# Loading one weight as mirrored 32x32 squares and turning it on VectorE, in a float32 two-layer sequence kernel

## The chip, the cores and the metric

The kernel runs on one core of one Trainium2 chip. Its time is the device time of one execution in microseconds; before the change it is the median of three executions, 1170.36 us. The engines are TensorE (PE, matrix products; PEld is its loading of the stationary operand), VectorE (DVE), ScalarE (ACT), GpSimd (POOL) and SyncE (SP, which here only issues transfers). Sixteen DMA engines move data between the chip's large memory and the on-chip memory of 128 partitions. SP, ACT and POOL each have a queue of transfers on these same sixteen engines.

## The reference

There are 4 sequences x of 512 tokens and 512 features, all in float32. The first layer, with V = 512 and HID = 2048:

```
q, k, v  = x @ Wq, x @ Wk, x @ Wv
attn     = softmax(q @ k.T * V**-0.5)
attn_out = (attn @ v) @ Wp + bp
cms      = gelu(attn_out @ cW1 + cb1) @ cW2 + cb2 + one_hot(code)
modifier = gelu([attn_out, cms] @ mW1 + mb1) @ mW2 + mb2
y        = clip(x + cms + modifier, 0, 1)
```

The second layer picks one of three small adapters for each sequence (`stream` is the index of the adapter):

```
h   = gelu(y @ W_down[stream] + b_down[stream]) @ W_up[stream] + b_up[stream]
out = layernorm(y + h) * ln_w[stream] + ln_b[stream]
```

## The kernel before

**Products by seven.** Every large product is cut into 2x2 blocks and computed with seven block products instead of eight (Winograd's form of Strassen's scheme). That needs four sums of the left operand's blocks (s1 to s4, made by `weight_sums`, L196) and four of the right operand's (t1 to t4). The wide products of the later layers use the scheme twice, one inside the other; their weights' sums (c1, c2, m1, m2) are made by GpSimd early in the kernel, in units, stored in the large memory and loaded again when their product comes. The generator `expansion` (L420) holds these units in order; `steps(expanding, n)` (L473) lets it issue the next n pieces.

**Attention.** The sequences are taken in two pairs. Wq and Wk are folded once into one matrix, Wq Wk^T, and Wv and Wp into another, Wv Wp (`folded`, L744). For each pair the code in L912 to L984 makes, in this order, u = x times the first matrix (`pair_product`, L933, both sequences at once), for the first pair the fold of Wv and Wp, two softmaxes (L773), two products that mix the rows of x by the attention (L970), and the product with the second matrix (L982). The results `attn` go to the large memory and come back as the right operand of c1, after which c2, m1, m2 and the adapters follow for each pair.

**The fold of Wv and Wp** needs Wv transposed, in `wv_t`, which is the tile mod[0], and four sums of its blocks, which take the place of the raw Wv in slot[2]. The raw Wv and Wp are loaded at the start by SP's queue, behind Wq and the first two x (L149 to L151). `then[7]` (L932) hangs the transposes of Wv into u's product, behind its block product p = 7: sixteen 128x128 transposes on TensorE into four banks of its accumulator memory (`transposed`, tile tr_ps, L489), each bank copied to wv_t by ScalarE and used by VectorE for the sums (`left_from_psum`, L720).

**u's product** takes the block products p in the order 1, 2, 5, 6, 7, 4, 3 for two row blocks r (`seven`, L591). After p = 6 and p = 7 VectorE adds kept results to the accumulators (L547): p = 4 goes into the accumulator of p = 7 and so cannot start on a row before VectorE's sum of p = 7 for that row has read it. The right operands of p = 5 and 6 lie in mod[0], those of p = 7 and 4 in mod[1].

**GpSimd's early work,** in its own order: the left sums of the first x (L923), the loads of the first half of cW1 (L234, four transfers) and of x 2 and 3 (L142), the first c1 unit, the right sums of Wp for the fold (L931, operations on L741), the rest of that unit, small constants (L524), the second c1 unit with the loads of cW2, and then the first c2 unit. The left sums of the second x stand in the program behind the first softmax (L951), since their place, wslot[0], holds a softmax operand until then; a scheduler, which orders each engine's instructions by estimated times, mixed them with the c2 unit. `tc.keep_in_program_order` pins an instruction against that scheduler; it is used for some groups of sums.

**Adapters.** `load_adapter` (L1486) fetches, by indirect transfers on GpSimd's queue, four pieces of W_down, two of b_down (bd), four of b_up (bu), two of W_up, and ln_w and ln_b for one sequence. It is called twice near the end of each pair. The bd and bu pieces have small tiles of their own, so nothing but their indices holds them back, and the scheduler put the first ones at 63 us and 22 more at 340 to 377 us. During c1 of the second pair GpSimd also makes sums of c1's right operands (L1079 and L1087 to L1090); in its queue they stand behind the first pair's adapter loads.

Of the kernel before, what the change touches and what calls it, by code (L numbers as in the profile page):

```python
# [1 line left out]

# [16 lines left out]
def kernel(  # L19
# [125 lines left out]
    def rows_of(t):  # L145
        return t.rearrange("p (c n) -> p c n", c=4)

    x_places = (big[0], big[1], rows_of(slot[6]), rows_of(slot[7]))
    x_rows = [load_x(b, nc.sync, x_places[b]) for b in range(2)]  # L149
    wv = weight((nc.sync, nc.sync), Wv, slot[2])  # L150
    wp = weight((nc.sync, nc.sync), Wp, slot[3])  # L151


    bias_src = (bp, cb1, cb2, mb1, mb2)
    counts = [v.shape[0] // P for v in bias_src]
# [37 lines left out]
        nc.tensor.matmul(idle_ps[:, :P], lhsT=zeros, rhs=zeros, start=True, stop=True)  # L193


    def weight_sums(a11, a12, a21, a22, s1, s2, s3, s4, eng=None):  # L196
        eng = eng or nc.gpsimd
        eng.tensor_tensor(s1, a21, a22, ALU.add)
        eng.tensor_tensor(s2, s1, a11, ALU.subtract)
        eng.tensor_tensor(s3, a11, a21, ALU.subtract)  # L200
        eng.tensor_tensor(s4, a12, s2, ALU.subtract)  # L201

    def token_sums(b11, b12, b21, b22, t1, t2, t3, t4, eng=None, pinned=False):
        eng = eng or nc.vector
# [144 lines left out]
    def expand(unit, raw, pairs, last, then):  # L349


        src, is_first, dst, u = unit
        raw = [t.rearrange("p (c n) -> p c n", c=4) for t in raw]
        a11, a12, a21, a22 = (
            raw[0][:, :, :256], raw[1][:, :, :256], raw[0][:, :, 256:], raw[1][:, :, 256:]
        )
        one, two, three = pairs
        s1, s2, s3 = (block(t[:, :1024]) for t in pairs)

        def tt(out_, a, b, op):  # L360
            nc.gpsimd.tensor_tensor(out_, a, b, op)

        def keep(p, t):
            nc.gpsimd.dma_start(out=dst[p, u], in_=t)

        tt(s1, a21, a22, ALU.add)
        tt(s2, s1, a11, ALU.subtract)
        tt(s3, a11, a21, ALU.subtract)

        def plain(*blocks):  # L370
            for p, a, t in blocks:
                inner_sums(a, t[:, 1024:])
                keep(p, t[:, 1024:])
                yield

        def fourth(s4, t):
            inner_sums(s4, t[:, 1024:])
            nc.gpsimd.dma_start(out=block(dst[3, u][:, :1024]), in_=s4)
            nc.gpsimd.dma_start(out=dst[3, u][:, 1024:], in_=t[:, 1024:])
            yield  # L380

        def full(*sums):
            for p, t in sums:
                inner_sums(block(t[:, :1024]), t[:, 1024:])
                keep(p, t)
                yield

        if last is not None:  # L390
            yield from plain((2, a12, one), (1, a11, three), (4, a22, two))
            tt(block(last), a12, s2, ALU.subtract)
            then()
            yield from full((5, one), (7, three), (6, two))
            yield from fourth(block(last), one)
        else:
            yield from plain((2, a12, one))
            tt(a12, a12, s2, ALU.subtract)
            yield from fourth(a12, three)
            yield from plain((1, a11, two), (4, a22, one))  # L400
            then()
            yield from full((5, one), (7, three), (6, two))
# [40 lines left out]
    def inner_weights(src, is_first, store, p, u):  # L443
# [26 lines left out]
            5: s[:, 0], 6: s[:, 1], 7: s[:, 2], 3: s[:, 3],  # L470
        }

    def steps(gen, n):  # L473
        for _ in range(n):
            next(gen, None)

    expanding = expansion()

# [186 lines left out]
        s1, s2, s3, s4 = (s[:, k] for k in range(4))  # L665
        return {1: a11, 2: a12, 3: s4, 4: a22, 5: s1, 6: s2, 7: s3}

    def left_sums(t, s):
        weight_sums(*halves(t), *(s[:, k] for k in range(4)))

    def right_operand(t, s):

# [43 lines left out]

    def sums_in(t):
        return t.rearrange("p (k c n) -> p k c n", k=4, c=2)

    def left_from_psum(t, s):  # L720

        s1, s2, s3, s4 = (s[:, k] for k in range(4))

        def finish(d, ps):
            nc.scalar.copy(t[:, d, :], ps)
            c = d % 2
            if d < 2:
                minus(s3[:, c], ps[:, :256], t[:, c, 256:])
            else:
                minus(s2[:, c], ps[:, 256:], s3[:, c])  # L730
                add(s1[:, c], ps[:, 256:], t[:, c, 256:])
                minus(s4[:, c], ps[:, :256], s2[:, c])

        return finish

    def right_sums(t, w):

# [174 lines left out]
    for pair in range(B // 2):  # L912
        s0, s1 = 2 * pair, 2 * pair + 1
        xT, t_x = places(pair)
        t_x = [sums_in(flat(t)) for t in t_x]
        u = big[4 - 2 * pair : 6 - 2 * pair]
        attn = big[6:8]
        s_u = [sums_in(wslot[k]) for k in range(2)]
        s_x = [sums_in(wslot[k]) for k in (2, 0)]
        t_p = t_x  # L920
        then = {}
        wv_t = mod[0]
        left_sums(x_rows[s0], s_x[0])  # L923
        if pair:
            s_x[1] = sums_in(flat(attn[1]))
            left_sums(x_rows[s1], s_x[1])
        if pair == 0:

            steps(expanding, 2)
            s_v = sums_in(slot[2])  # L930
            rhs_wp = right_sums(wp, w_vp)  # L931
            then[7] = [lambda: transposed(chunks(wv), wv_t, left_from_psum(wv_t, s_v))]  # L932
        pair_product(lhs_qk, begun, u, beside=beside_u(s_u, u), then=then)  # L933
        if pair == 0:

            lhs_vp = folded(
                left_operand(wv_t, s_v), rhs_wp, w_vp, s_v, order=(1, 5, 6, 2, 7, 3, 4)
            )
        steps(expanding, 6 if pair else 4)
        pT, mix = u, xT  # L940

        def turn(k):
            transposed(lambda t: mod[k][:, t, :], pT[k], right_from_psum(pT[k], t_p[k]))

        for k in range(2):
            softmax(
                k, left_operand(u[k], s_u[k]), right_operand(xT[k], t_x[k]),
                {7: [lambda: turn(0)]} if k else None,
            )
            if k == 0 and pair == 0:  # L950
                left_sums(x_rows[s1], s_x[1])  # L951
        for k in range(2):
            if k == 0:
                def keep(half, tokens, ps):
                    nc.scalar.copy(
                        mix[0][:, 2 * half : 2 * half + 2, 256 * tokens : 256 * tokens + 256], ps
                    )
            else:
                operands, take = second_operand(*mix, mod)
                held = []  # L960

                def keep(half, tokens, ps):

                    if (half, tokens) == (1, 1):
                        held.append(ps)
                        return
                    take(half, (slice(0, 2), slice(256 * tokens, 256 * tokens + 256)), ps)
                    if (half, tokens) == (0, 1):
                        take(1, (slice(0, 2), slice(256, 512)), held[0])

            small_product(
                left_operand(x_rows[s0 + k], s_x[k]), right_operand(pT[k], t_p[k]), keep,
                {7: [lambda: turn(1)]} if k == 0 else None,
                nc.scalar.copy if k else nc.vector.tensor_copy,
            )
            steps(expanding, 6)
        then = {}
        if pair == 0:
            begun = {}
            then = {6: [lambda: first_operand(1)()], 4: [lambda: begun.update(both_operands(1))]}  # L980

        pair_product(lhs_vp, operands, attn, bp_c, then=then, at=pT[0] if pair else None)  # L982
        for k in range(2):
            nc.scalar.dma_start(out=attn_kept[s0 + k], in_=attn[k])  # L984
# [489 lines left out]
    bd_rows = b_down.rearrange("e (k o) -> (e k) o", o=1)  # L1474

    def gathered(dst, rows, idx):
        nc.gpsimd.indirect_dma_start(
            out=dst,
            out_offset=None,
            in_=rows,  # L1480
            in_offset=bass.IndirectOffsetOnAxis(ap=idx, axis=0),
        )
# [3 lines left out]
    def load_adapter(b, w, aff):  # L1486
        wd = w[:, : NV * BN].rearrange("p (c n) -> p c n", c=NV)
        wu = w[:, NV * BN : NV * BN + NB * V].rearrange("p (c n) -> p c n", c=NB)
        aff = aff[:, : 2 * V].rearrange("p (k n) -> p k n", k=2)
        bd = small.tile([P, NB], F32, name="bd")  # L1490
        bu = small.tile([P, NV], F32, name="bu")
        for c in range(NV):
            gathered(wd[:, c, :], wd_rows, idx_d[:, b, c : c + 1])
        for c in range(NB):
            gathered(bd[:, c : c + 1], bd_rows, idx_u[:, b, c : c + 1])
        for c in range(NV):
            gathered(bu[:, c : c + 1], bu_rows, idx_d[:, b, c : c + 1])
        for c in range(NB):
            gathered(wu[:, c, :], wu_rows, idx_u[:, b, c : c + 1])
        for i, rows in enumerate((ln_w, ln_b)):  # L1500
            gathered(aff[:, i, :], rows, idx_e[:, b : b + 1])
        return wd, wu, bd, bu, aff

    def with_bias(y, bu, y1):
# [297 lines left out]
```

## Time and profile before

| | |
|---|---|
| Three timed runs | 1168.99, 1170.36, 1171.34 us |
| Median | 1170.36 us |
| Profiled execution, its own time | 1169.93 us |
| Its span in the profile | 1168.2 us |
| TensorE busy, matrix products | 1158.7 us (99%) |
| VectorE busy | 893.8 us (77%) |
| ScalarE busy | 293.2 us (25%) |
| GpSimd busy | 588.6 us (50%) |
| Transposes of Wv on TensorE (tr_ps, 16) | 42.9 to 48.8 us of the span |
| Left sums of the second x on GpSimd | 95.9 to 111.8 us |
| Bias gathers on GpSimd, longest run | 339.7 to 377 us |

The profile follows one execution. Times are microseconds from the start of its span. A group or a row names the line of the kernel, the engine, the operation and its tiles (out<-in); "idle before" is how long the engine had stood still and what ended that. The chain of waits is followed back from the last instruction: at each step to what released it, or to the instruction before it on its engine. A matrix product of float32 with 256 columns appears as two records.

### The profile page before, as it was taken

How to read it: one execution, taken by the hardware profiler on the slowest of the kernel's cores; microseconds unless marked ns; L12 is line 12 of the kernel's file. 1: busy time of each engine (PE TensorE's matmuls, PEld its weight loads, DVE VectorE, ACT ScalarE, POOL GpSimd, SP SyncE). 2: the span in 40 equal slices, each digit the busy share in tenths (PEclk: the TensorE clock that was granted, in tenths of full speed). 3: DMA queues.
4: the chain of work that ended last, by engine and by line, in shares of the span. 5: the costliest groups of instructions: out<-in, count | busy, mean ns of one | idle time of the engine just before them, and what ended most of it. 6: DMA issues, size and time to landing. Idle time of an engine off the chain costs nothing.

```text
span 1168.2 us, 13723 instructions
## 1 busy us (share of the span) xinstructions
PE 1158.7 (99%) x4989; PEld 927.4 (79%) x4989; DVE 893.8 (77%) x1215; ACT 293.2 (25%) x535; POOL 588.6 (50%) x652
## 2 busy tenths in 40 slices
PE   9999999999999999999999999999999999999997
PEld 8588558657468888888888887778888888888875
DVE  5755655587699967899699956689994588689956
ACT  4244315236520000012310027271000003220014
POOL 4989999988897058982200636972000001242101
PEclk9999999999999999999999999999999999999999
DMA  9742784897766588896847662135745454594701
GB/s 336 268 139 100 297 323 176 307 382 253 300 240 245 185 282 313 322 328 263 258 157 279 191 215 90 64 143 179 299 132 188 168 216 180 176 307 165 246 6 73
DMA packets 81283, 256.80 MB, mean 220 GB/s; under 512 B 7956, under 2 KB 38976, under 8 KB 65984
## 3 DMA queue, kind: packets, MB, share of 16 engines
q1 hardware_dynamic: 56864, 152.98, 36.4%
q0 software_dynamic: 21968, 93.37, 22.7%
q10 hardware_dynamic: 2384, 9.57, 2.1%
q8 instruction: 40, 0.66, 0.2%
q14 instruction: 27, 0.22, 0.1%
HBM read 186.69 MB, written 66.06 MB: 216 GB/s over the span
## 4 chain that ended last, share of the span: by engine, by line
PE 94%; DVE 2%; POOL 1%; DMA 1%; issue 1%; DVEq 0%
PE i L1406 29%; PE i L1306 26%; PE sum L1148 9%; PE sum L703 9%; PE sum L637 8%; PE c L1238 6%; PE down_ps L1512 2%; PE up_ps L1531 2%; PE tr_ps L489 1%; DMA wslot<-in_L_cond_mW 1%; PE up_ps L1526 1%; DVE slot L206 1%; DVE hidden L547 1%; PE tr_ps L868 0%; PE idle_ps L193 0%
## 5 line engine op out<-in xcount | busy, mean ns | idle before, releaser
L1306 PE MATMUL i<-slot,wslot 128*128 128x256 f32 x1184 | 261.4, 379 | 1.3 <-DVE part L1010 1.2
L1306 PEld LDWEIGHTS i<-slot,wslot 128*128 128x128 f32 x1184 | 224.7, 190 | 32.8 <-issue 1.8
L1406 PE MATMUL i<-slot,wslot 128*128 128x256 f32 x896 | 202.5, 379 | 0.0
L1406 PEld LDWEIGHTS i<-slot,wslot 128*128 128x128 f32 x896 | 170.2, 190 | 23.1
L1017 ACT COPY first<-i 128x256 f32<-128x256 f32 (+1 forms) x56 | 26.7, 477 | 516.0 <-PE i L1406 255.6
L1406 PE MATMUL i<-hidden,wslot 128*128 128x256 f32 x576 | 132.2, 379 | 0.0
L1406 PEld LDWEIGHTS i<-hidden,wslot 128*128 128x128 f32 x576 | 109.4, 190 | 15.7 <-issue 1.0
L1010 DVE TENSOR_TENSOR part<-i,part 128x512 f32<-128x512 f32 (+1 forms) x156 | 90.5, 591 | 37.7 <-PE i L1306 25.4
L1039 ACT ACTIVATE hidden<-hidden,bias 128x512 f32<-128x512 f32 x128 | 83.9, 716 | 81.3 <-DVE hidden L547 71.3
L1688 POOL DMA_DIRECT2D slot<-xT_kept x4 | 2.7, 683 | 152.9 <-PE i L1306 152.9
L1148 PE MATMUL sum<-mod,wslot 128*128 128x256 f32 x288 | 66.7, 379 | 0.2 <-DVE sum L547 0.2
L206 DVE TENSOR_TENSOR slot<-hidden 128x1024 f32<-128x1024 f32 x46 | 61.3, 1332 | 0.0
L1148 PEld LDWEIGHTS sum<-mod,wslot 128*128 128x128 f32 x288 | 54.6, 190 | 7.9 <-DVE sum L547 0.6
L1691 POOL TENSOR_TENSOR cms<-cms,slot 128x512 f32<-128x512 f32 x16 | 24.4, 1548 | 71.3 <-PE i L1306 41.1
L1010 DVE TENSOR_TENSOR part<-i,first 128x512 f32<-128x512 f32 (+1 forms) x62 | 36.3, 589 | 29.0 <-PE i L1306 17.7
L547 DVE TENSOR_TENSOR sum<-sum,wslot 128x512 f32<-128x512 f32 x48 | 33.3, 696 | 31.5 <-PE sum L703 19.6
L206 DVE TENSOR_TENSOR slot<-hidden,slot 128x1024 f32<-128x1024 f32 x46 | 56.8, 1234 | 0.3
L1238 PE MATMUL c<-slot,wslot 128*128 128x512 f32 x128 | 55.3, 592 | 0.0
L547 DVE TENSOR_TENSOR hidden<-part,hidden 128x2048 f32<-128x2048 f32 x20 | 54.6, 2732 | 0.5
L703 PE MATMUL sum<-hidden,wslot 128*128 128x256 f32 x232 | 53.4, 380 | 0.6 <-POOL wslot L201 0.6
L703 PEld LDWEIGHTS sum<-hidden,wslot 128*128 128x128 f32 x232 | 43.7, 190 | 6.7 <-POOL wslot L201 1.0
L1238 PEld LDWEIGHTS c<-slot,wslot 128*128 128x128 f32 x128 | 24.3, 190 | 30.6 <-issue 27.5
(338 smaller groups left out, 2129.3 us busy)
## 6 DMA issues: line engine op xcount, KB each, us to landing
wslot<-m_kept SPq DMA_DIRECT2D x48, 1024.0 KB
wslot<-m_kept SPq DMA_DIRECT2D x36, 512.0 KB
wslot<-c_kept SPq DMA_DIRECT2D x16, 1024.0 KB
slot<-in_L_cond_mW POOLq DMA_DIRECT2D x24, 512.0 KB
wslot<-in_L_cond_mW SPq DMA_DIRECT2D x24, 512.0 KB
wslot<-in_L_cond_cW SPq DMA_DIRECT2D x40, 256.0 KB
slot<-in_L_cond_cW POOLq DMA_DIRECT2D x16, 512.0 KB
m_kept<-wide POOLq DMA_DIRECT2D x6, 1024.0 KB
```

Source lines behind the costliest of these rows:

```text
L206: i = eng.tensor_tensor(out_, one, two, ALU.subtract)
L547: nc.vector.tensor_tensor(dst, a, b, ALU.add)
L637: nc.tensor.matmul(ps, lhsT=lhs[p][:, c, r * P : (r + 1) * P], rhs=rhs[p][:, c, :], start=(first_ and c == 0), stop=(c == 1), skip_group_c ...
L703: nc.tensor.matmul(v[:, j, :], lhsT=lhs[p][:, c, j * P : (j + 1) * P], rhs=rhs[p][:, c, :], start=(first_ and j == 0 and c == 0), stop=(c ...
L1010: nc.vector.tensor_tensor(dst, ps, other, ALU.add)
L1017: nc.scalar.copy(c1, p1)
L1039: nc.scalar.activation(block[:, t, :], block[:, t, :], AF.Gelu, bias=bias_c[:, 8 * half + t : 8 * half + t + 1],)
L1148: nc.tensor.matmul(halves_of(ps)[:, j, :], lhsT=a[g][:, at_[q], j * P : (j + 1) * P], rhs=rhs[q][:, 0, :], start=(first_ and j == 0), stop ...
L1238: nc.tensor.matmul(ps, lhsT=lhs(c, t), rhs=operands[p][:, c, :], start=(c == 0), stop=(c == 1),)
L1306: nc.tensor.matmul(out_ps[:, j, :], lhsT=a[j][q][:, c, :], rhs=now[q][:, c, :], start=(c == 0), stop=(c == 1),)
L1406: nc.tensor.matmul(ps[:, :256], lhsT=a[k // 2][q][:, k % 2, :], rhs=now[q][:, k, :], start=(k == 0), stop=(k == 3),)
L1691: nc.gpsimd.tensor_tensor(cms[s][:, d, :], cms[s][:, d, :], in_rows[3][:, d, :], ALU.add)
```

## The change

There are four edits.

1. Wv is loaded after Wp instead of before it, with four transfers of 32 partitions, one for each group of partitions, on SP's queue (`load_squares`). Each places 32x32 squares so that block (i, j) of Wv stands where block (j, i) was; a contiguous piece is 32 numbers, 128 bytes, so 8192 pieces in place of 512 of 2 KB. VectorE then turns all squares in place of TensorE's sixteen transposes: one `transpose` of 128x2048 from slot[2] to wv_t, which completes the transposed matrix, and the four left sums of 128x512, also on VectorE. `left_from_psum` and its copies on ScalarE go.
2. The right sums of Wp are issued ahead of the expansion's first two steps, with high priority.
3. The left sums of the second x of a pair are followed by the expansion's next steps: `steps` opens with `tc.issue_after` the last of those sums, so that none of the next unit's instructions is put ahead of them. For the first pair the first sum is pinned in program order.
4. The bd and bu gathers, and the other later ones of `load_adapter`, are issued after the first W_down gather of the same adapter.

In the compiled order, GpSimd's right sums of Wp stand behind the first of the four cW1 loads and mixed with the last left sum of the first x; the left sums of the second x stand directly behind the second c1 unit, ahead of the constants and of the c2 unit; in the second pair they stand directly behind those of the first x. The 24 bias gathers stand behind the first four W_down gathers of their adapters. On VectorE the turn stands behind the sums of p = 6 and ahead of the sum of p = 7 for row block 0.

```diff
+    def load_squares(src, dst, eng):
+        squares = src.rearrange("(i r) (d a c) -> a r d i c", r=32, a=4, c=32)
+        for a in range(4):
+            eng.dma_start(
+                out=dst[32 * a : 32 * a + 32].rearrange("p d (i c) -> p d i c", c=32),
+                in_=squares[a],
+            )
...
-    wv = weight((nc.sync, nc.sync), Wv, slot[2])
     wp = weight((nc.sync, nc.sync), Wp, slot[3])
+    wv = rows_of(slot[2])
+    load_squares(Wv, wv, nc.sync)
...
+    behind = []
+
     def steps(gen, n):
-        for _ in range(n):
-            next(gen, None)
+        with tc.issue_after(behind.pop().ins) if behind else nullcontext():
+            for _ in range(n):
+                next(gen, None)
...
         left_sums(x_rows[s0], s_x[0])
         if pair:
             s_x[1] = sums_in(flat(attn[1]))
-            left_sums(x_rows[s1], s_x[1])
+            behind.append(left_sums(x_rows[s1], s_x[1]))
         if pair == 0:
+            with tc.high_priority():
+                rhs_wp = right_sums(wp, w_vp)
             steps(expanding, 2)
             s_v = sums_in(slot[2])
-            rhs_wp = right_sums(wp, w_vp)
-            then[7] = [lambda: transposed(chunks(wv), wv_t, left_from_psum(wv_t, s_v))]
+            def turn_wv():
+                nc.vector.transpose(wv_t, wv)
+                left_sums(wv_t, s_v, nc.vector)
+            then[7] = [turn_wv]
...
             if k == 0 and pair == 0:
-                left_sums(x_rows[s1], s_x[1])
+                behind.append(left_sums(x_rows[s1], s_x[1], pinned=True))
...
-        for c in range(NV):
-            gathered(wd[:, c, :], wd_rows, idx_d[:, b, c : c + 1])
-        for c in range(NB):
-            gathered(bd[:, c : c + 1], bd_rows, idx_u[:, b, c : c + 1])
+        start = [gathered(wd[:, c, :], wd_rows, idx_d[:, b, c : c + 1]) for c in range(NV)][0]
+        with tc.issue_after(start.ins):
+            for c in range(NB):
+                gathered(bd[:, c : c + 1], bd_rows, idx_u[:, b, c : c + 1])
...
```

`weight_sums` returns its last instruction and can pin its first; `left_sums` passes an engine and the pin on to it; `gathered` returns its instruction.

## The prediction

> **What bounds the kernel now.** I read the totals first, then TensorE's list of waits, the chain of work around the change, and the DMA's share by stretches. The profiled execution took 1169.93 us, with a span of 1168.2; the median of the three timed runs is 1170.36, or 0.43 more.
>
> ```profile
> PE 1158.7 (99%) x4989; PEld 927.4 (79%) x4989; DVE 893.8 (77%) x1215; ACT 293.2 (25%) x535; POOL 588.6 (50%) x652
> ...
> PE 94%; DVE 2%; POOL 1%; DMA 1%; issue 1%; DVEq 0%
> ```
>
> TensorE is busy for 1158.7 of 1168.2 us and is 94% of the chain that ended last. A change gains only if it takes work from TensorE or removes one of its waits; it loses whatever new wait it gives TensorE.
>
> ```profile
> PE i L1306 <- DVE part L1010: 1.2, 1, 1.2
> ...
> PE sum L703 <- POOL wslot L201: 0.6, 1, 0.6
> ```
>
> Of these two waits the change touches the second: TensorE waits once for a left sum that GpSimd makes late. The chain shows where, and shows the transposes that go:
>
> ```profile
> 25.05 18.03 PE sum L637 x42
> 43.08 0.87 PE tr_ps L489 x8
> 43.95 1.72 PE sum L637 x4
> 45.67 0.44 PE tr_ps L489 x4
> 46.11 2.58 PE sum L637 x6
> 48.68 0.44 PE tr_ps L489 x4
> 49.12 1.72 PE sum L637 x4
> ...
> 110.56 1.29 POOL wslot L201
> 111.85 0.04 issue
> 111.89 3.72 PE sum L703 x16
> ```
>
> The columns are start, length and what ran. The 16 transposes of Wv stand inside the product u = lhs_qk x, and nothing else runs on TensorE meanwhile.
>
> **What is removed.** Transposes: 0.87 + 0.44 + 0.44 = 1.75 us of TensorE, all on the chain. The four copies of 0.59 us on ScalarE (L725) and 12 VectorE operations of 0.41 us go too; both engines have idle time there, so I count nothing for them. The wait at 111.3: 0.58 us. Removing only the transposes would have made that wait 0.58 + 1.75 = 2.33 us, because GpSimd does not follow TensorE there; so the gain depends on the second part of the change. Together: -2.33 us.
>
> **The left sums.** GpSimd now makes the sums of the second sequence's x straight after the unit c1(1), before the constants and the cW2 unit. By its own times that is: c1(1) ran from 65.6 to 82.5 plus two operations, the constants and two gathers before it (57.3 to 65.6, 8.3 us) now come later, so the four sums of 1.27 us start at about 75.5 and end near 80.6. Their place wslot[0] is free when softmax(0) has read it, which is before softmax(1) takes over at about 73. TensorE wants them from 102.5 on: 20 us of cover, priced at nothing. In pair 1 the same sums move from 200.8 to about 165; they are wanted after 207.
>
> **The right sums of Wp** (L741, 4 x 1.27 us) move on GpSimd from 46.4 to about 17.5, past three of the four c1 loads and both x loads. Each of these DMAs is issued 5.0 us later (18.7 becomes 23.7), and the first c1 unit, which began at 29.1, can begin up to 5.0 later; the 5.0 us come back where the sums stood. x is wanted at 129, c1's results after 219. Nothing on the chain.
>
> **The bias gathers** (bd, bu) lose their early places (63 to 65.6 and 339.7 to 377, where GpSimd afterwards idles 35 us) and join the other gathers of each adapter: 12 more in the run from 654.5 to 677.1. Price each at 37.3/22 = 1.7 us: 20 us. Behind them in GpSimd's queue stand the c1 operand sums (L1087, 679.8 before), now near 697 to 700. TensorE reads these at 709.3, so 9 us of cover remain; without it each gather would cost its 1.7 us. In the last pair the runs at 1035 and 1070 grow by 10 us each and end before 1100; wanted at 1118.7 to 1146. Nothing.
>
> **VectorE's turn.** The compiled order puts it after the two sums of p = 6 and ahead of the sum of p = 7, row 0. These are their times before (start, length, and idle before it):
>
> ```profile
> 38.82 0.70 DVE L547 TENSOR_TENSOR sum<-sum,wslot 128x512 f32<-128x512 f32 x1 [0.85 <-PE sum L637]
> 40.54 0.70 DVE L547 TENSOR_TENSOR sum<-sum,wslot 128x512 f32<-128x512 f32 x1 [1.02 <-PE sum L637]
> ```
>
> The turn can start at 39.42. No transpose by VectorE is in this trace. Bounds: 1.2 us (a 128x1024 sum, if it ran at twice the rate) and 4.6 (twice a 128x2048 sum of 2.28); I take 2.28, the row with its shape. The delayed sum then ends at 39.42 + 2.28 + 0.70 = 42.40. TensorE ends p = 7 at 42.07, has one product of p = 3 (0.86) in hand, and needs the sum at 42.93: 0.5 us to spare. At 4.6 it would wait 1.8.
>
> **Wv's arrival.** This is the term that decides. The turn waits for all of Wv, and everything behind it on VectorE waits too. If Wv lands at L, TensorE waits L + 2.28 + 0.70 - 42.93 = L - 39.95 us.
>
> ```profile
> 20.00:27.00 7.00, 7.00 (x36) 5.18 (x35) 5.76 (x13) 3.81 (x7) 2.44 (x4) 1.00 1.03 387
> 27.00:37.00 10.00, 10.00 (x25) 4.46 (x24) 9.43 (x21) 2.34 (x4) 7.89 (x9) 1.00 1.02 399
> 37.00:42.00 5.00, 5.00 (x13) 2.19 (x12) 2.37 (x4) 0.58 (x1) 4.98 (x6) 1.00 0.08 31
> ```
>
> The last two columns are the DMA engines' busy share and GB/s. They are full until 37 + 0.08 x 5 = 37.4 us, then empty to 42. Wv was 512 pieces of 2 KB: 1.05 MB at 395 GB/s = 2.65 us. Now it is 8192 pieces of 128 bytes, 512 for each engine, and goes last on SP's queue, behind Wp, which ends where Wv ended before: by 12.0 us 264 GB/s had moved Wq, Wk and the first x (3.15 MB), and two more MB at 2.65 us make 17.3. From there it shares the engines with GpSimd's loads. How they share is seen at 287 to 290, when both queues have work:
>
> ```profile
> q0 software_dynamic: 199, 0.70, 66.1%
> q1 hardware_dynamic: 198, 0.36, 37.4%
> ```
>
> Packet for packet, 199 to 198, whatever their size. GpSimd's and ScalarE's queues have 64 to 80 packets for each engine left by then, Wv has 512; so Wv ends last, when all the work is done: L = 37.4 - 2.65 + 512c + 1.0, where c is one piece's time and 1.0 the lag to the waiter (the first x had moved by 12.0, its reader on GpSimd starts at 12.99). For c, the trace's packet records give 15 ns (median of 32 records of 128 bytes in a copied constant; their mean is 269, stalled behind others), 27 ns for 512 bytes, 47 for 1 KB, 84 for 2 KB. I take 15, the row of the same size: L = 43.4, a wait of 3.5 us, and the sum is -2.33 + 3.5 = +1.15. The ends: none of the wait if pieces go ahead of their turn (-2.33); 47 ns, the smallest piece that this queue carries now, gives L = 59.8 and +17.5; 27 ns gives L = 49.6, a wait of 9.6, +7.3.
>
> Two rules of the Trainium skill bear on this, and they pull apart. "DMA: Bandwidth & Descriptors", Specifications, says that transfers below 512 bytes are not at line rate because they are read, modified and written back; with 512 bytes' 27 ns the sum would be +7.3. The same page, "Queues, rings and completion order", says an engine drains a packet of some 9 to 17 descriptors before it turns to another queue; then Wv would end well before 39.95, and the sum would be -2.33. The 199 to 198 above speaks against the second.
>
> **Forecast: about no change,** 1169.93 + 1.15 + 0.43 = 1171.5 against 1170.36. Its own range, c from 12.8 to 17.3 ns, is 1170.4 to 1172.7.
>
> **Rivals.** *Wv comes in time*: full gain, 1170.36 - 2.33 = 1168.0. For it: Wv has the engines nearly alone from 17.3 to 25, as GpSimd's loads start 5 us later. At c below 12 ns it fits. Against it: packet-for-packet sharing. *The small pieces are dear* (slower): VectorE stands at the turn while Wv trickles in, TensorE stops at p = 4; above 12.8 ns the change loses, above 17.3 by more than 0.2%; at 27 ns, 1177.7. For it: records rise from 15 to 27 ns within the sizes next to it, and no load from HBM here has pieces this small. *The gathers are dearer*: at 3.0 us each, the dearest of the run at 339.7, they take 36 us, the sums come at 716 and TensorE waits 7 us: 1175 with the full gain. It decides from 2.4 us each; the mean of 1.7 speaks against it.
>
> **How the numbers follow.** Differences under 0.2% (2.3 us) count as none; the three runs lie 2.35 apart. Forecast 0.34, Wv in time 0.32, dear pieces 0.29, gathers or another new wait 0.05. In time lies on the bound of 0.2%: 0.18 of it faster, 0.14 same. Of the forecast 0.28 same, 0.06 slower; the others slower. Faster 0.18, same 0.42, slower 0.40. The range runs from 1167.3 (full gain and the runs' scatter) to 1178.5 (27 ns and scatter).
>
> **What would show it.** VectorE's wait in front of the turn names a DMA of Wv and ends near 43 (forecast), is absent (gain), or ends past 45 (slower); TensorE's list has a wait at L637 of the same length less 0.5; the wait at L703 for GpSimd is gone; L1148 has no new wait near 709. A turn much longer than 2.3 us, or a wait for GpSimd after 640, would make the prediction wrong.

## The result, and the profile after

Fourteen timed runs of the changed kernel have a median of 1171.74 us (1169.14 to 1175.34), against 1169.01 (1167.68 to 1171.34) of the kernel before: ratio 1.0021, interval 1.0011 to 1.003. That is slower by 0.2%, at the edge of what can be told. The forecast was 1171.5, from a base of 1170.36. The profiled execution took 1171.24 us, its span is 1169.1 (before: 1168.2).

The totals, then TensorE's list of waits (us in total, how often, the longest):

```profile
PE 1156.0 (99%) x4973; PEld 925.5 (79%) x4973; DVE 893.0 (76%) x1212; ACT 290.8 (25%) x531; POOL 589.1 (50%) x652
```

```profile
PE sum L648 <- DVE sum L558: 3.4, 1, 3.4
PE i L1306 <- DVE part L1010: 1.4, 1, 1.4
PE idle_ps L202 <- DVE zeros L199: 1.1, 1, 1.1
```

The 16 transposes are gone (x4989 to x4973), and so is the wait for GpSimd's left sum. In their place stands a wait of 3.4 us that was not there before, for the sum of p = 7. VectorE's timeline around it (start, length; in brackets the idle time before and what ended it):

```profile
38.64 0.70 DVE L558 TENSOR_TENSOR sum<-sum,wslot 128x512 f32<-128x512 f32 x1 [0.85 <-PE sum L648]
43.34 2.31 DVE L930 STREAM_TRANSPOSE mod<-slot 128x2048 f32<-128x2048 f32 x1 [4.00 <-DMA slot<-in_L_cond_Wv]
45.58 0.67 DVE L558 TENSOR_TENSOR sum<-sum,wslot 128x512 f32<-128x512 f32 x1
```

The turn stands in VectorE's queue behind p = 6 and waits for Wv until 43.34. The sum of p = 7 is free of Wv, but behind the turn. TensorE at the same time:

```profile
41.87 1.02 PE L648 MATMUL sum<-hidden,wide 128*128 128x512 f32 x2
46.30 3.70 PE L648 MATMUL sum<-mod,cms 128*128 128x512 f32 x8 [3.41 <-DVE sum L558]
```

The stretches shown before, again with the DMA engines' busy share and GB/s in the last two columns, and under them the queues at 31 to 39 us (packets, MB, share):

```profile
20.00:27.00 7.00, 7.00 (x36) 5.14 (x36) 5.76 (x14) 3.81 (x7) 7.00 (x9) 1.00 1.19 289
27.00:37.00 10.00, 10.00 (x25) 4.42 (x24) 9.43 (x20) 2.34 (x4) 6.38 (x9) 1.00 1.01 366
37.00:42.00 5.00, 5.00 (x13) 2.22 (x12) 1.49 (x3) 0.00 (x0) 5.00 (x5) 1.00 1.08 326
```

```profile
q0 software_dynamic: 554, 2.14, 67.3%
...
q1 hardware_dynamic: 562, 0.07, 5.9%
```

The engines are now full until 42, and GpSimd's queue (q0) and Wv's (q1) move one packet each in turn, 554 to 562, although one is 4 KB and the other 128 bytes. Equal counts alone would also fit longer turns, but at 38 to 39 us, when only these two queues are busy, 90 of the 91 pieces of Wv have a 4-KB packet starting 8 to 20 ns after their own start. A piece of 128 bytes took 13 ns (median of the packet records). The first three quarters of Wv are in by 27.1. The last 2048 pieces start near 30.5; until 39 some 560 of them pass, and at 39 to 42, as GpSimd's queue has only 190 packets more, 1372 do. The last one ends at 43.0.

The chain that ended last, from 9 us on, shows a part that nothing before showed:

```profile
9.35 9.33 SPq L152
...
18.73 3.78 SPq L152
...
22.56 20.76 DMA slot<-in_L_cond_Wv
...
43.34 2.31 DVE mod L930
```

SP is held 9.33 us in handing over the second quarter, so the fourth is handed over only at 26.

### The profile page after: what moved, and what is told of

The parts are those of the page before. It is cut to its first block, busy times and chain, and to the rows that moved or that the text cites. A ratio compares the mean times of both kernels' runs of the same rounds, so it can differ in the third digit from the quotient of the medians.

```text
span 1169.1 us, 13695 instructions
## 1 busy us (share of the span) xinstructions
PE 1156.0 (99%) x4973; PEld 925.5 (79%) x4973; DVE 893.0 (76%) x1212; ACT 290.8 (25%) x531; POOL 589.1 (50%) x652
## 4 chain that ended last, share of the span: by engine, by line
PE 93%; DMA 3%; DVE 2%; SPq 1%; issue 0%; ACTq 0%; DVEq 0%
PE i L1406 29%; PE i L1306 26%; PE sum L714 9%; PE sum L1148 9%; PE sum L648 7%; PE c L1238 6%; PE down_ps L1512 2%; PE up_ps L1531 2%; DMA slot<-in_L_cond_Wv 2%; SPq L152 1%; DMA wslot<-in_L_cond_mW 1%; PE tr_ps L500 1%; DMA wide<-in_L_cond_Wk 1%; DVE hidden L558 1%; PE up_ps L1526 1%; DVE slot L217 1%
## 5 line engine op out<-in xcount | busy, mean ns | idle before, releaser
L358 POOL DMA_DIRECT2D slot<-in_L_cond_mW x24 | 17.8, 750 | 80.1 <-DVE slot L217 79.1
L217 DVE TENSOR_TENSOR slot<-hidden 128x1024 f32<-128x1024 f32 x46 | 56.9, 1238 | 0.0
```

What stands on the lines that cost most here:

```text
L217: i = eng.tensor_tensor(out_, one, two, ALU.subtract)
```

## The experiments

My theory: the wait is Wv's arrival, set by sharing with GpSimd's loads, and it strikes only because of where the turn stands. Rivals: SP's slow handing over sets the arrival; VectorE's new work costs the time wherever it stands; the new order on GpSimd costs it.

The table sums up all runs. "Lead" is how far TensorE stands ahead (-) or behind (+) of the kernel before in the profiled executions, each weight load matched with its like in the other trace, counted from 30 us on so that the start's jitter is left out: at the first product of the fold, at 64 us, and at 112 us, behind the place of the old wait. The last column is TensorE's half clock around an idle time, from the trace's clock records (start of its first window); the half clock at the very end of every trace is left out.

| kernel | ratio (interval) | lead at fold | at 64 | at 112 | half clock |
|---|---|---|---|---|---|
| changed, first profile | 1.0021 (1.0011-1.003) | +1.92 | +1.92 | +1.07 | none |
| changed, once more | 1.0023 (1.0012-1.0035) | +3.10 | +3.10 | +2.26 | 3.41 us at 46.7 |
| turn behind p = 4 | 0.9997 (0.9988-1.0006) | -1.27 | -0.91 | -1.75 | none |
| x loads later | 0.9992 (0.9982-1.0002) | -1.76 | -1.76 | -2.60 | none |
| old Wv, new GpSimd order | 0.9995 (0.9986-1.0004) | 0.00 | 0.00 | -0.84 | none |
| turn behind p = 7 | 0.9994 (0.9985-1.0003) | -1.75 | -0.82 | -1.67 | none |
| turn behind p = 7, x later | 0.9998 (0.9986-1.001) | -1.76 | -1.13 | -1.97 | none |
| same turn, left sums put back | 0.9989 (0.998-0.9998) | -1.75 | -0.74 | -1.58 | 3.41 us at 265.8 |
| that one again | 1.0109 (1.0093-1.0126) | -1.75 | -1.75 | -2.60 | 10.24 us at 685.4 |
| last quarter loaded twice | 1.0047 (1.0033-1.0062) | +5.25 | +5.60 | +4.75 | 3.41 us at 50.8 |
| all of GpSimd put back | 1.0018 (1.0008-1.0029) | -1.75 | +4.34 | +3.49 | 3.41 us at 56.4 |
| only right sums early | 1.0003 (0.9993-1.0013) | -1.76 | -1.33 | -2.17 | none |
| Wv ahead of Wp | 1.0137 (1.0117-1.0157) | -0.61 | +0.33 | -0.51 | 13.65 us at 685.1 |

**The changed kernel once more**, unaltered.

> The changed kernel once more, unaltered, for a second trace of Wv's arrival. My theory (Wv's last pieces share the DMA engines packet for packet with GpSimd's loads): TensorE waits 3 to 5 us at L648 for VectorE's sum, the turn starts at 43 to 45 us, the span is 1169 to 1171, and the time 0.15 to 0.3% above the kernel before; the arrival may move by 1 us or more with the order in which the engines serve the queues, and this is what scatters its times. Rival (the arrival is set by how fast SP hands the pieces over): the turn starts at 43.3 again within 0.3 us, and the scatter comes from elsewhere.

Ratio 1.0023; the turn starts at 42.99, 0.35 from the first profile. Between these two traces the arrival hardly moves, so they do not show that it scatters the times, as my theory had it; two traces don't rule it out either (with the same early loads, runs below have Wv's last piece at 41.7 to 43.7). But TensorE's timeline and the clock (the third column from the right, granted share) show something else:

```profile
45.95 5.40 PE L648 MATMUL sum<-mod,cms 128*128 128x512 f32 x8 [2.89 <-DVE sum L558]
51.18 2.74 PE L648 MATMUL sum<-hidden,wide 128*128 128x512 f32 x6
```

```profile
44.00:46.00 2.00, 0.05 (x1) 0.05 (x1) 2.00 (x3) 0.07 (x1) 1.98 (x3) 1.00 0.59 170
46.00:48.00 2.00, 2.00 (x3) 0.77 (x4) 2.00 (x4) 1.10 (x2) 2.00 (x4) 0.66 0.77 223
48.00:50.00 2.00, 2.00 (x4) 0.96 (x3) 2.00 (x3) 0.00 (x0) 2.00 (x4) 0.50 1.04 317
```

The wait is shorter (2.89), yet the eight matmuls behind it take 5.40 us and not 3.70: behind the idle time the clock is halved for 3.41 us, which costs 1.7 us. The first profile, with 3.41 us idle, has none of it.

**The turn behind the sums of p = 4.**

```diff
+                    added.append(add(x[r], x[r], c1[r]))
...
+                with tc.issue_after(added[-1].ins):
+                    nc.vector.transpose(wv_t, wv)
...
-            then[7] = [turn_wv]
+            then[4] = [turn_wv]
```

> Everything of the change is kept; only VectorE's turn of Wv is ordered behind the sums of p = 7 and p = 4, so that no sum of the product u stands behind it. My theory: Wv lands at 43.3 as before, the turn starts there, but TensorE no longer waits in the product u; the fold, which would start at 49.1, has its operand at 45.7 and the first sum at 46.4. The whole gain of 2.33 us shows: span near 1165.9, ratio 0.998, and the scatter of the times falls to that of the kernel before (some 4 us). Rival (turning Wv on VectorE and its sums cost what was lost, wherever they stand): the wait moves to the fold (L714) and the ratio stays at 1.001 to 1.003.

Wv's last piece ends at 41.7 in this run. The wait in the product u is gone and the loss with it: ratio 0.9997. The gain falls short of 0.998, for the turn came too late:

```profile
46.41 0.69 DVE L558 TENSOR_TENSOR sum<-sum,wslot 128x512 f32<-128x512 f32 x1
47.01 2.30 DVE L931 STREAM_TRANSPOSE mod<-slot 128x2048 f32<-128x2048 f32 x1
```

It waited for the sums of p = 4 until 47.01, and the fold began 0.5 us later than it could.

**The loads of the third and fourth x later.**

```diff
-        for b in range(2, B):
-            x_rows.append(load_x(b, nc.gpsimd, x_places[b]))
         yield from expand_c1(0, lambda: load_c1(1))
+        for b in range(2, B):
+            x_rows.append(load_x(b, nc.gpsimd, x_places[b]))
```

> Everything of the change is kept; only the loads of the third and fourth x (1.05 MB each, GpSimd's queue) are issued behind the first unit of c1 instead of ahead of it. My theory (sharing packet for packet): 2.1 MB less stands beside Wv, at 395 GB/s 5.3 us, so Wv lands near 38, the turn starts behind the sums of p = 6 at 39.4, TensorE waits under 0.6 us at L648; span near 1166, ratio 0.998. Rival (SP's handing over, or the small pieces' own time, sets the arrival): the turn still starts near 43 and the ratio stays at 1.001 to 1.003.

Wv's last piece ends at 36.55, 6.5 us earlier, though SP hands over the fourth quarter at the same time as ever (22.98, 3.38 us long). The last quarter's pieces start near 30, as in the changed kernel. So SP's handing over may set when the last quarter starts, but the sharing sets how long it takes, and the 6.5 us are the sharing's. The stretches, DMA share and GB/s last:

```profile
27.00:37.00 10.00, 10.00 (x25) 4.47 (x24) 9.43 (x22) 3.00 (x6) 7.17 (x9) 1.00 0.85 260
37.00:42.00 5.00, 5.00 (x13) 2.18 (x12) 4.15 (x6) 0.00 (x0) 5.00 (x5) 1.00 0.26 107
```

```profile
40.28 2.30 DVE L930 STREAM_TRANSPOSE mod<-slot 128x2048 f32<-128x2048 f32 x1
42.51 0.67 DVE L558 TENSOR_TENSOR sum<-sum,wslot 128x512 f32<-128x512 f32 x1
```

The turn follows p = 6 at once, still ahead of the sum of p = 7, and TensorE loses nothing: the full lead of 2.60 us at 112. In the timed runs 0.9992 is left of it.

**Wv as before, the rest of the change kept** (rows of 2 KB ahead of Wp, 16 transposes, copies on ScalarE).

```diff
-    wp = weight((nc.sync, nc.sync), Wp, slot[3])
-    wv = rows_of(slot[2])
-    load_squares(Wv, wv, nc.sync)
+    wv = weight((nc.sync, nc.sync), Wv, slot[2])
+    wp = weight((nc.sync, nc.sync), Wp, slot[3])
...
-            then[7] = [turn_wv]
+            then[7] = [lambda: transposed(chunks(wv), wv_t, left_from_psum(wv_t, s_v))]
```

> Wv is loaded and turned as before (rows of 2 KB, ahead of Wp; 16 transposes and their copies); GpSimd's new order of left sums, right sums and gathers is kept. My theory: the 16 transposes are back at 1.75 us, the wait of 0.58 us for GpSimd's left sum is gone, nothing else changes: span 1167.6, ratio 0.9995 (0.9985 to 1.0005). Rival (the new order on GpSimd costs somewhere, for example by the stalls of its stores at 56 and 65 us): ratio 1.001 or more although the wait for Wv is gone.

0.9995 as expected. The lead is nothing until 64 and 0.84 at 112: the old wait, listed with 0.58, was worth 0.84. The new order on GpSimd costs nothing here.

**The turn right behind the sums of p = 7** (as above with p = 7, and then[7] kept).

> As the changed kernel, but VectorE's turn is ordered right behind the two sums of p = 7 (not behind those of p = 4 as in the run before, where it started only at 47.0 and held up the fold). My theory: the turn starts when Wv lands, 43.0 to 43.4, ends by 45.7, ahead of the fold at 49.1; no wait in the product u, no wait in the fold, so TensorE is 1.75 us ahead of the kernel before at the fold and 2.3 ahead behind the old wait at 111 us; the granted clock stays full after 40 us. Ratio 0.9975 to 0.999. Rival (VectorE's turn and four sums cost TensorE something wherever they stand): less than 1.2 us ahead at 57 us, ratio 0.9995 or more.

The turn starts at 43.16, and the fold 1.75 us ahead, so the transposes are worth what was counted. Then 0.9 is lost again in the fold. VectorE's sums of Wv, and TensorE:

```profile
46.55 1.21 DVE L211 TENSOR_TENSOR slot<-mod 128x512 f32<-128x512 f32 x1
47.69 1.61 DVE L210 TENSOR_TENSOR slot<-slot,mod 128x512 f32<-128x512 f32 x1
...
49.56 0.87 DVE L212 TENSOR_TENSOR slot<-mod,slot 128x512 f32<-128x512 f32 x1
```

```profile
56.98 1.96 PE L714 MATMUL sum<-cms,slot 128*128 128x256 f32 x8 [0.69 <-DVE sum L558]
```

These sums take 0.67 us at their shortest and up to 1.61 here (what slows them was not tested), and the fold waits for the sums queued behind them. The rival was half right. Ratio 0.9994.

**Both: turn behind p = 7 and x later.**

> The turn right behind the sums of p = 7, and the loads of the third and fourth x behind the first unit of c1. My theory: Wv lands near 39, the turn starts at 42.8 as soon as the last sum of p = 7 is done, full gain, ratio 0.9975 to 0.999, with scatter as in the kernel before. If the arrival in the run with the turn alone moved is sometimes later than 46 us, this one is the faster; else the two are the same within 0.1%. Rival (later loads of x cost later): slower than the run with the turn alone by 0.1% or more.

0.9998, not told apart from the run before it; two of its twelve times lie at 1172.8 and 1174.7. No sum of the two gains.

**The left sums put back**, turn behind p = 7.

```diff
-            behind.append(left_sums(x_rows[s1], s_x[1]))
+            left_sums(x_rows[s1], s_x[1])
...
-                behind.append(left_sums(x_rows[s1], s_x[1], pinned=True))
+                left_sums(x_rows[s1], s_x[1])
```

> The turn right behind the sums of p = 7, and the left sums of each second sequence's x back where they were before the change, that is behind the constants and the unit of cW2. My theory (step of the prediction: without the second part the wait of 0.58 us grows by the 1.75 that TensorE saves): TensorE waits 2.3 us for GpSimd's left sum near 110 us, and the whole gain is gone: ratio 0.9995 to 1.0005. Rival (GpSimd would be early enough without that part): no wait at L714 for GpSimd, ratio 0.998.

There is no wait for GpSimd, and the lead at 112 is as with the sums moved. GpSimd's last left sum:

```profile
105.40 1.27 POOL L212 TENSOR_TENSOR wslot<-hidden,wslot 128x512 f32<-128x512 f32 x1
```

It ends at 106.7 and not at 111.8: the compiled order has put it ahead of other work by itself. My theory fell here. The same profile shows a second place with a wait and a half clock:

```profile
255.08 7.78 DVE L217 TENSOR_TENSOR mod<-wide,mod 128x256 f32<-128x256 f32 x1
```

```profile
264.72 2.76 PE L1148 MATMUL sum<-mod,wslot 128*128 128x256 f32 x8 [2.33 <-DVE sum L558]
267.27 2.86 PE L1148 MATMUL sum<-slot,wslot 128*128 128x256 f32 x8
```

A sum of 128x256, 0.41 us elsewhere, lasted 7.78 while GpSimd ran three sums of 128x1024 one after the other; TensorE idled 2.33 us, and eight matmuls then took 2.86 us, not 1.89. With the turn alone moved the same sum lasted 5.46 and nothing waited. So such waits come and go between executions.

**The last quarter of Wv loaded twice**, the turn ahead of both sums of p = 7.

```diff
-        for a in range(4):
+        for a in (0, 1, 2, 3, 3):
...
+            then[6] = [lambda: hold.append(nc.vector.transpose(wv_t, wv))]
```

> The turn is ordered ahead of both sums of p = 7, and the last quarter of Wv (2048 pieces) is loaded a second time behind the first, so that TensorE must stand idle longer: Wv complete at 48 to 52, an idle time of 6 to 10 us. My theory (an idle TensorE loses clock: after 2.9 us idle the second profile of the changed kernel shows half clock for 3.41 us, 1.7 us lost; the first profile, after 3.4 us, does not): with so long an idle time the half clock shows for certain, 3.41 us or a multiple, and costs 1.7 us or more on top of the idle time. Rival (the slow stretch had nothing to do with the wait): no half clock between 40 and 70 us, and the product runs on at 0.22 us for each matmul of 128x512 at once.

Wv is complete at 48.2 (the turn starts at 48.90), TensorE idles 5.35 us (short of the 6 to 10 expected), and the half clock is there, for 3.41 us from 50.8:

```profile
52.00:54.00 2.00, 2.00 (x4) 0.88 (x3) 2.00 (x4) 1.01 (x2) 0.00 (x0) 0.50 1.06 432
54.00:56.00 2.00, 2.00 (x6) 1.04 (x5) 1.03 (x3) 0.12 (x1) 0.17 (x1) 0.96 0.92 379
```

Ratio 1.0047.

**Everything on GpSimd put back**, squares and the turn behind p = 7 kept (left sums, right sums without their priority, gathers as before).

> Only the squares of Wv and VectorE's turn (right behind the sums of p = 7) are kept; on GpSimd the left sums, the right sums of Wp and the bias gathers are asked for where they were before the change. View of the prediction: GpSimd does not follow TensorE, its last left sum ends at 111.8 and TensorE, 1.5 to 1.8 us earlier there, waits 2.0 to 2.3 us for it: ratio 0.9995 to 1.0005. Rival, from the run with the left sums alone put back (no such wait, sum done at 106.7): the compiled order puts the sums earlier by itself once the 16 transposes and their copies are gone, about 108.4, no wait at L714 for GpSimd; ratio 0.998 to 0.9995, and the three edits on GpSimd are worth nothing beside it.

There is no wait for GpSimd's left sum, but TensorE comes 4.3 us late there, so that is no test of the prediction's view. The sum ends at 109.96 and not at 111.8, so here too the compiled order moved it. And 1.0018 is not "worth nothing". GpSimd's loads begin 5 us earlier, SP is held 14.6 us with the third quarter, Wv's last piece ends at 45.35, and the fold waits:

```profile
46.14 2.31 DVE L930 STREAM_TRANSPOSE mod<-slot 128x2048 f32<-128x2048 f32 x1 [3.22 <-DMA slot<-in_L_cond_Wv]
...
50.63 2.43 DVE L211 TENSOR_TENSOR slot<-mod 128x512 f32<-128x512 f32 x1
```

```profile
56.13 3.50 PE L714 MATMUL sum<-cms,slot 128*128 128x256 f32 x8 [3.26 <-DVE wslot L569]
```

The sums of Wv are slow here too, 1.75 and 2.43 us; how much of the 3.26 us is theirs and how much is Wv's late arrival was not separated. Moving the right sums ahead, which I priced at nothing, holds GpSimd's loads back and so lets Wv in earlier; the next run tests it.

**Only the right sums early** (left sums and gathers as before).

> Squares of Wv, the turn right behind the sums of p = 7, and the right sums of Wp early as in the change; the left sums and the bias gathers where they were before it. Against the run with everything on GpSimd put back it differs in the right sums alone. My theory: the early right sums hold back GpSimd's loads by 5 us, so Wv lands at 42 to 43.5 again and not at 45.4; the turn starts by 43.6; no wait of 3.3 us in the fold at 53 to 56 (at most 0.8 us for VectorE's sums), clock full; the last left sum ends near 108 to 110 and TensorE, which wants it at 110.4, waits under 0.5 us; with only 16 gathers in the run from 650 us they end near 678, and no wait at L1148 near 684 as in the two runs of the last call that kept 28 there. Ratio 0.9985 to 0.9997. Rival (the loss in the fold came from the right sums running beside VectorE's sums, not from Wv's arrival): Wv lands at 45.4 again. Rival for the late part (the stall near 684 is not the gathers' doing): it shows here too.

Wv's last piece ends at 42.0, 3.3 us earlier than in the run above, from which it differs in the right sums alone. The fold loses 0.4 us, and TensorE leads by 2.17 us at 112; the last left sum ends at 109.70, just in time. The late part shows no wait. The ratio is 1.0003 all the same: the profiled execution, at 1167.2, is the fastest of twelve with a median of 1169.37.

**Wv ahead of Wp.**

```diff
+    wv = rows_of(slot[2])
+    load_squares(Wv, wv, nc.sync)
     wp = weight((nc.sync, nc.sync), Wp, slot[3])
-    wv = rows_of(slot[2])
-    load_squares(Wv, wv, nc.sync)
```

> The changed kernel with Wv's squares handed over ahead of Wp instead of behind it. My theory (sharing one for one with GpSimd's loads, which begin near 24): Wv's 8192 pieces, 512 for each engine at 13 ns or 6.7 us in all, start at 12 with nothing but ScalarE's and SP's rests beside them and land before 30, far ahead of the turn; no wait at L648 above 1 us, full clock; ratio 0.9985 to 1.000. What it may cost: Wp comes later and GpSimd's right sums with it, but the fold wants them only at 49. Rival (SP's blocked handing over, 17.5 us for the four transfers, sets the arrival): last piece not before 8.6 + 17.5 + 3.5 + 9 = 38, as the fourth transfer is handed over at 26 and trickles.

A miss. Three quarters are in by 21.9, but the fourth, handed over by 21.0, starts near 26.5, when GpSimd's queue is busy, and ends at 40.4; what holds its start back by 5 us was not found. The median is 15.6 us higher, and in the trace 12.6 us of the loss come at another place, near 684:

```profile
PE sum L1148 <- DVE sum L558: 9.4, 2, 7.3
```

**The run with the left sums put back, again.**

> The run with the left sums put back and the turn behind the sums of p = 7 once more, since it had the lowest ratio so far (0.9989, interval 0.998 to 0.9998): if it is truly faster than the kernel before, the ratio comes out at 0.998 to 0.9995 again; if that was luck of the waits behind VectorE at 260 and 500 us, it comes out at 0.9995 to 1.0005.

Neither: 1.0109, on another chip than the first time, with the same kernel and a larger lead at 112. It is the same place near 684. VectorE there:

```profile
683.55 0.70 DVE L558 TENSOR_TENSOR sum<-sum,mod 128x512 f32<-128x512 f32 x1 [1.38 <-remote]
689.18 0.70 DVE L558 TENSOR_TENSOR sum<-sum,mod 128x512 f32<-128x512 f32 x1 [4.94 <-remote]
```

VectorE starts up to 4.9 us late without any engine of the trace as the releaser, TensorE waits 8.3 us for it in two pieces, and its clock is halved for 10.24 us. GpSimd is issuing its 28 gathers at that time (651.9 to 690.0). The kernel with everything on GpSimd put back, on the same chip, issues 16 there, ends at 678.9 and has no such stall. That points to the gathers; but kernels with 28 gathers on two other chips have none either, so what makes it is left open, and whether the changed kernel meets it on that chip was not tried.

## Why the prediction was right, and where it was not

*Transposes, -1.75:* right; the fold begins 1.75 us ahead wherever nothing waits.

*The old wait, gone:* right, and worth 0.84 instead of 0.58, so that the full gain is 2.60 and not 2.33. "GpSimd does not follow TensorE there; so the gain depends on the second part" was wrong: with the left sums put back the last one ended at 106.7, 109.7 or 110.0 instead of 111.8, since the compiled order changed with the rest.

*Left sums:* they came at 83.6 to 88.6 instead of 75.5 to 80.6, behind two stalls for stores that I had not counted (4.81 and 5.19 us). The cover of 14 us was enough.

*Right sums of Wp:* at 17.6 to 23.8 as computed, and the first unit 2 us late. But the move was not neutral: without it Wv comes 2.3 to 3.3 us later and the fold stands still.

*Gathers:* 28 in 39.0 us, 1.4 us each, and the c1 sums at 694.5 instead of 697. Free in the two profiles of the changed kernel. The third rival put its wait near 709, for sums that come late on GpSimd. The stall near 684 in two other runs is a wait for VectorE; its cause is open.

*The turn:* 2.31 us against 2.28, and with Wv in time TensorE loses nothing to it, as the 0.5 us to spare said.

*Wv's arrival:* 43.34 against 43.4, the wait 3.41 against 3.5. That Wv ends with the whole traffic was right: the DMA engines' busy share is 0.18 at 42 to 43 us and 0 at 43 to 44. That the times agree to 0.1 us is in part luck: the piece cost less (13 ns, not 15), which in the formula gives 42.4, and the fourth quarter came later to the queue than I thought. The rule of the Trainium skill ("DMA: Bandwidth & Descriptors", Queues, rings and completion order) on draining 9 to 17 descriptors at a time is not what the packet records show, if each record is one descriptor: 554 against 562, singly in turn at 38 to 39 us. That transfers under 512 bytes are not at line rate (Specifications) agrees: 128 bytes in 13 ns are 9.8 GB/s on one engine, 4 KB in 159 ns 25.8. It did not make the pieces dear in time.

*The sum, +1.15:* the mechanism was right, and a term was left out, the clock. The first trace stands 1.07 us behind at 112, as predicted; the timed runs lost 2.2 to 2.7 us by their medians. That 1171.74 lies so near to 1171.5 is luck: the base of three runs, 1170.36, was 1.35 above the median of fourteen, about as much as the missing term. The mean granted clock of the single runs points to the rest: 0.9976 over 26 runs of the changed kernel, 0.9989 over 35 of the kernel before. The difference is 1.5 us of 1168, and one half-clock window costs 1.7: by this estimate nearly nine runs in ten have one, and 1.07 + 0.9 x 1.7 = 2.6. Of the 26, the four at 0.999 took 1170.0 us on average, the eighteen at 0.997 and 0.998 1171.5, the four at 0.996 or less 1173.8. Where the half clock lay in the 24 runs without a trace is not known.

"TensorE: Matmul & The Clock Gate", Part 1, of the Trainium skill says that the clock falls to half after an idle window of about 3.4 us, counted in free-running windows. The half and the 3.41 us agree here; but idle times of 2.33 and 2.89 us were enough, and one of 3.41 was not followed by it. The traces show why: in each, the clock changes only at steps of 3.413 us from the first clock record (the half clock at 46.66 comes twelve steps after 5.70). In the fourteen traces, between the start and the very end, each such window at full clock that held 2.14 us or more of idle TensorE was followed by half clock (six traces), and none that held 1.99 or less was. The first profile's 3.41 us fell across two windows, 1.99 and 1.42 us. Where the wait falls in the windows so decides; by this, an idle time of 2.9 to 3.4 us would meet half clock in some six to eight executions of ten, an estimate somewhat under the one above.

What stays open: with the wait removed, TensorE leads by 1.6 to 2.6 us at 112, but the timed runs gain between -0.4 and 1.3. By the estimate above, their mean granted clocks, 0.9983 to 0.9988, make 0.1 to 0.6 us of it. Waits behind VectorE at 262 and near 500 us, 0 to 2.3 us from one execution to the next, lie between; I have not shown that they take it. No version is shown to be faster than the kernel before on more than one chip: the turn pinned behind p = 7 (0.9994) and the later x loads (0.9992) undo the change's loss, and the 0.9989 did not hold on another chip.

## What to carry to other kernels

An instruction that waits for a late transfer must not stand in an in-order queue ahead of sums that need nothing of it: order it behind the last sum that TensorE is waiting for. A transfer in many small packets that shares engines packet for packet with large ones can, as here, end only when all the traffic ends; moving the large loads brought it in 6.5 us earlier. And price a new wait of TensorE of 2 us or more with the clock that it may lose behind it: here 1.7 us for each window, in six of the seven traces with such a wait.

## What the runs showed of the hardware beyond that

SP's queue shows the four quarters of Wv, 2048 pieces each, as one line (start, length):

```profile
8.59 17.48 SPq L152 DMA_DIRECT2D slot<-in_L_cond_Wv  x4
```

Wp's two halves take 0.97 us to hand over, these four 17.48. With everything on GpSimd put back, one quarter alone holds SP for 14.56 us. In most runs the last quarter's pieces still began only 3 to 5 us after the handing over (0.8 us with everything on GpSimd put back). And half-clock times came in whole windows of 3.41 us: one, three (10.24) or four (13.65).
